# A two-layer graph network on one core: POOL keeps only row transfers in the first part, ScalarE copies the weights, VectorE adds the bias of q, and node pieces come at a ratio of 1.4

## The chip, the core and the metric

One core of a Trainium2 chip runs the whole program. TensorE is called PE, VectorE DVE, ScalarE ACT, GpSimd POOL and SyncE SP. Each engine works through its own instruction list strictly in order and waits for the others by semaphores. The metric is the device time of one execution in microseconds (us).

## The reference, cut to what matters

There are 6250 nodes with 256 features each, and 100000 edges sorted by their destination. Layer 0 is a typed attention: every node has one of three types, every edge one of six relations.

```python
h = relu(layernorm(x))
k, q, v = typed_linear(h, Wk, bk), typed_linear(h, Wq, bq), typed_linear(h, Wv, bv)   # weights of the node's type
k_rel = einsum('nhd,rhde->rnhe', k, rel_att)      # 6 relations, 4 heads
v_rel = einsum('nhd,rhde->rnhe', v, rel_msg)
att = (q[dst] * k_rel[edge_type, src]).sum(-1) * rel_pri[edge_type] / sqrt(64)
# softmax over the edges of one (destination, relation), weighted sum of v_rel, mean over relations
# then: typed linear, skip, layernorm, residual; layer 1 is a GAT on the same edges, batchnorm, elu, residual
```

The change is in the part that makes q, k_rel and v_rel for all nodes while the edges are sorted.

## The kernel before, in words

The first part does two things side by side. `sort_edges` (line 619) sorts the edges by destination and relation, almost wholly on DVE: exchanges of minimum and maximum (lines 686 and 687) in rows of an array, and, from step k = 8 on, in its columns as well. Between the two layouts the array is turned by seven PE transposes (`turn`, line 710, transposes at line 713). The sort is a Python generator: it yields a cost after each group of steps, and right after issuing a `turn`.

`node_stage` (line 588) handles the nodes in blocks of 128 rows that are sorted by node type, 51 blocks (SB). It is a generator too. One turn of its loop has five pieces, each ending in a `yield` with its cost. I call them A to E:

- A: gather the rows of a block eleven ahead (`take_rows`, POOL, line 482), copy a block's k and v weights to a fixed place (`take_weights`, POOL, line 490), the row statistics on DVE (`row_scales`, `row_stats`), and `relate(s, 0)`.
- B: `relate(s, 1)`. C: `keys_values(s + 1)`, 16 matmuls (line 543) and four ACT evictions (line 549). D: `relate(s, 2)`.
- E: `relate(s, 3)`, ending in the scatter of the block's k_rel and v_rel rows to memory (POOL, line 447); the normalized rows of block s + 3 (ACT, line 522); the transpose of block s + 2 (line 530); and `queries(s + 1)`: two PE products (line 557) into a PSUM bank, the copy of the bank by ACT (line 562), the addition of the bias by POOL (line 563), and the scatter of the q rows (line 447).

Each `relate` is eight matmul records on PE (line 577, for two parts together) and one ACT copy of 128x768 from PSUM (line 578). `bank()` gives PSUM banks from a pool of two: keys_values, the transpose and the queries use them in turn.

The order of the work is the order in which this Python code issues it (`tc.manual_schedule()`): nothing is reordered in the first part. The two generators are woven by this loop at line 893, in which RATE sets how many node pieces follow each group of sort steps:

```python
        RATE = 1.13
        due = done = 0.0
        for cost in sort_edges():
            due += cost * RATE
            while done < due:
                part = next(nodes, None)
                ...
                done += part
        ...
        for _ in nodes:          # what is left of the nodes
            pass
```

So in every engine's list the order around one turn is: the transposes of the turn, then the node pieces that are due, then the sort steps that work on what was turned. I call that a segment. There are 24 turns. The message stage after it (`chain`, `bulk`, lines 1034 and 1216) loads the q rows back into `QA` (`load_queries`, line 942), whose memory is also the staging room of k_rel and v_rel, and gathers from `kv_d`: it needs all nodes and the whole sort.

Of the kernel before, what the change touches and what calls it, by code (L numbers as in the profile page):

```python
# [8 lines left out]
F32 = mybir.dt.float32  # L9
# [3 lines left out]
OP = mybir.AluOpType  # L13
# [4 lines left out]
P = 128  # L18
# [6 lines left out]
def kernel(  # L25
# [29 lines left out]
    nc = tc.nc  # L55
    N, D = x.shape
# [4 lines left out]
    FC = D // P  # L61
# [159 lines left out]
    with ExitStack() as st:  # L221
# [4 lines left out]
        nwork = st.enter_context(tc.tile_pool(name="nwork", bufs=2))  # L226
# [5 lines left out]
        def bank():  # L232
            return ps_n.tile([P, 512], F32, name="nps")
# [50 lines left out]
        w_s = nconst.tile([P, FC, T, 3, D], F32, name="w_s")  # L284
# [5 lines left out]
        bq_s = nconst.tile([P, T, D], F32, name="bq_s")  # L290
# [88 lines left out]
        for t in range(2, T):  # L379
# [20 lines left out]
            op=OP.is_equal,  # L400
# [7 lines left out]
        for j in range(0, NX, 7):  # L408
# [5 lines left out]
                op=OP.is_equal,  # L414
# [30 lines left out]
        def scatter(table, to, index, key):  # L445

            i = nc.gpsimd.indirect_dma_start(  # L447
                out=table,
                out_offset=bass.IndirectOffsetOnAxis(ap=index, axis=0),
                in_=to,  # L450
                in_offset=None,
                bounds_check=table.shape[0] - 1,
                oob_is_err=False,
            )
            tc.declare_no_dep(i.ins, group=key, reason="each row is written once")
            tc.add_to_no_dep_group(key, i.ins)


        GN = 4
        xbs, mvs, rss, hqs, hTs, ws, kvs, kinds = {}, {}, {}, {}, {}, {}, {}, {}  # L460
        PE, POOL = mybir.EngineType.PE, mybir.EngineType.Pool

        def kind_of(b, engine):
            if (engine, b) not in kinds:
                n = min(8, SB - b)
                _, ks = nc.values_load_multi_w_load_instructions(
                    kind_i[0:1, b : b + n],
                    engines=[engine],
                    min_val=0,
                    max_val=T - 1,  # L470
                    skip_runtime_bounds_check_because="a block is of one of T types",
                )
                kinds.update({(engine, b + i): k for i, k in enumerate(ks)})
            return bass.ds(kinds[engine, b], 1)

        def there(b):
            return 0 <= b < SB

        def take_rows(b):
            if there(b):  # L480
                xbs[b] = nwork.tile([P, D], F32, name="xb", bufs=10)
                nc.gpsimd.indirect_dma_start(
                    out=xbs[b], out_offset=None, in_=x[:, :],
                    in_offset=bass.IndirectOffsetOnAxis(ap=from_row[:, b : b + 1], axis=0),
                )

        def take_weights(b):
            if there(b):
                ws[b] = nwork.tile([P, FC, 2, D], F32, name="w_now")
                nc.gpsimd.tensor_copy(  # L490
                    ws[b].rearrange("p c i d -> p c (i d)"),
                    w_s[:, :, kind_of(b, POOL), 1:, :].rearrange("p c a i d -> p c (a i d)"),
                )

        def row_stats(b):
            if not there(b):
                return
            g, i = b // GN, b % GN
            if i == 0:
                mvs[g] = nwork.tile([P, GN, 2], F32, name="mv_n", bufs=3)  # L500
                rss[g] = nwork.tile([P, 2, GN], F32, name="rs_n", bufs=3)
            st = nwork.tile([P, nc.vector.BN_STATS_DIM], F32, name="st_n")
            nc.vector.bn_stats(out=st, in_=xbs[b])
            nc.vector.bn_aggr(out=mvs[g][:, i, :], in_=st)
            if i == GN - 1 or b == SB - 1:
                nc.scalar.activation(rss[g][:, 0, : i + 1], mvs[g][:, : i + 1, 1], AF.Sqrt, bias=eps_t)

        def row_scales(b):
            if there(b) and b % GN == 0:
                n = min(GN, SB - b)  # L510
                rs, mv = rss[b // GN], mvs[b // GN]
                nc.vector.reciprocal(rs[:, 0, :n], rs[:, 0, :n])
                nc.vector.scalar_tensor_tensor(
                    rs[:, 1, :n], mv[:, :n, 0], -1.0, rs[:, 0, :n], op0=OP.mult, op1=OP.mult
                )
# [18 lines left out]
        def keys_values(b):  # L534

            if not there(b):
                return
            kv = bank().rearrange("p (i n) -> p i n", n=P)
            w = ws.pop(b)
            for i in range(2):  # L540
                for c in range(FC):
                    for ci in range(FC):
                        nc.tensor.matmul(
                            kv[:, i * FC + c, :], w[:, ci, i, c * P : (c + 1) * P], hTs[b][:, ci, :],
                            start=(ci == 0), stop=(ci == FC - 1),
                        )
            kvs[b] = nwork.tile([P, 2 * FC, P], F32, name="kvT")
            for i in range(2 * FC):
                nc.scalar.activation(kvs[b][:, i, :], kv[:, i, :], AF.Identity, bias=bias_c[:, i, b : b + 1])

        def queries(b):
            if not there(b):
                return
            q = bank()[:, :D]
            hT = hTs.pop(b)
            for c in range(FC):
                nc.tensor.matmul(
                    q, hT[:, c, :], w_s[:, c, kind_of(b, PE), 0, :].rearrange("p a d -> p (a d)"),
                    start=(c == 0), stop=(c == FC - 1),
                )  # L560
            hq = hqs.pop(b)
            nc.scalar.copy(hq[:, 1, :], q)
            nc.gpsimd.tensor_tensor(
                hq[:, 1, :], hq[:, 1, :], bq_s[:, kind_of(b, POOL), :].rearrange("p a d -> p (a d)"), op=OP.add
            )
            scatter(hq_d[:, :], hq.rearrange("p i d -> p (i d)"), to_row[:, b : b + 1], "hq")

        def relate(b, part):

            if not there(b):  # L570
                return
            i, c = part // FC, part % FC
            rel = room[:, b % 4 * RB : (b % 4 + 1) * RB].rearrange("p (r i h e) -> p r i h e", r=R, i=2, h=H)
            ps = ps_r.tile([P, 2, 512], F32, name="rps")[:, :, : R * DK].rearrange("p a (r e) -> p a r e", r=R)
            for a in range(2):
                rows = slice(a * DK, (a + 1) * DK)
                nc.tensor.matmul(ps[:, a], kvs[b][rows, i * FC + c, :], (ra_s, rm_s)[i][rows, c], start=True, stop=True)  # L577
            nc.scalar.copy(rel[:, :, i, 2 * c : 2 * c + 2, :].rearrange("p r h e -> p h r e"), ps)  # L578
            if part == 3:
                del kvs[b]  # L580
                scatter(
                    kv_d.rearrange("(n r) d -> n (r d)", r=R),
                    room[:, b % 4 * RB : (b % 4 + 1) * RB],
                    to_row[:, b : b + 1],
                    "kv",
                )

        def node_stage():

            for s in range(-11, SB):  # L590
                take_rows(s + 11)
                take_weights(s + 2)
                row_scales(s + 3)
                row_stats(s + 9)
                relate(s, 0)
                yield 0.9 * there(s)
                relate(s, 1)
                yield 0.9 * there(s)
                keys_values(s + 1)
                yield 2.1 * there(s + 1)  # L600
                relate(s, 2)
                yield 0.9 * there(s)
                relate(s, 3)
                norm_rows(s + 3)
                turn_rows(s + 2)
                queries(s + 1)
                yield 0.9 * there(s) + 0.45 * there(s + 2) + 1.1 * there(s + 1)

        nodes = node_stage()

        for n in (3, 3, 0, 0, 0, 0, 1, 1, 4, 4, 4):
# [278 lines left out]
            )  # L890
            nc.vector.tensor_tensor(dl0, keyc, dlf[:, :NT], op=OP.mult)

        RATE = 1.13
        due = done = 0.0
        for cost in sort_edges():
            due += cost * RATE
            while done < due:
# [81 lines left out]
    with ExitStack() as st:  # L979
# [4 lines left out]
        op = st.enter_context(tc.tile_pool(name="a0o", bufs=2))  # L984
# [469 lines left out]
    with ExitStack() as st:  # L1454
# [5 lines left out]
        op = st.enter_context(tc.tile_pool(name="b1o", bufs=2))  # L1460
# [270 lines left out]
        with tc.manual_schedule():  # L1731
# [19 lines left out]
            for c in range(DENSE):  # L1751
                ahead = chain(c + 1) if c + 1 < DENSE else iter(())
                soon = destination_scores(c + 2) if c + 2 < DENSE else iter(())
                for j in range(C):
                    t = c * C + j
                    i = t // GT
# [40 lines left out]
    with ExitStack() as st:  # L1797
# [71 lines left out]
        for k in range(PC):  # L1869
            for c in range(FC):  # L1870
                d = hT[:, c, k * PW : (k + 1) * PW]
                nc.vector.tensor_scalar(d, d, mu[:, c : c + 1], None, op0=OP.subtract)
        for k in range(PC):
            for c in range(FC):
                d = hT[:, c, k * PW : (k + 1) * PW]
# [87 lines left out]
```

## Time and profile before

| | us |
|---|---|
| median of 3 runs | 3434.46 (3433.5 to 3435.92) |
| the profiled execution, its own time | 3434.26 |
| its span | 3432.4 |
| first turn of the sort begins | 139.8 |
| last sort instruction on DVE ends (L891) | 430.8 |
| last scatter of k_rel and v_rel leaves POOL (L447) | 496.1 |
| first product of the message stage on PE (L1074) | 545.9 |

The profile's times count from the start of its span. A row of the waits names the engine and line that waited, what released it, the total, the number of waits and the longest. A row of the timeline has start, duration, engine, line, operation and, in brackets, the idle time before it. The granted clock of PE (PEclk) is a share of full speed.

### The profile page before, as it was taken

Reading aid. Unit: us, or ns where it says so; the run is one execution under the profiler, and the core shown is the slowest. Engines: PE = TensorE matmul, PEld = TensorE weight load, DVE = VectorE, ACT = ScalarE, POOL = GpSimd, SP = SyncE. Lnnn points to the kernel's source line nnn. Section 1 sums busy time; section 2 is a strip of 40 time slices with the busy share of each in tenths; the row PEclk is TensorE's granted clock in tenths of the full one; section 3 lists DMA queues with packets and bytes.
Section 4 is the critical chain, followed back from the end, with each engine's and each line's share of the span. In section 5 each row is a group of like instructions: output and inputs, shape, how many; then the busy total and the mean of one; then the engine's idle time right before and its main releaser. Section 6 shows DMA issues by size and latency. Waiting matters only on the chain. (4 is left out here: it accounts for less than half of the span.)

```text
span 3432.4 us, 45921 instructions
## 1 busy us (share of the span) xinstructions
PE 2286.5 (67%) x9977; PEld 1621.8 (47%) x9977; DVE 2431.4 (71%) x5405; ACT 1924.1 (56%) x7430; POOL 2138.1 (62%) x2156
## 2 busy tenths in 40 slices
PE   3888874787777777777776775265555555655554
PEld 2555543555555555555544664144333334434343
DVE  8999714898888989889876886255555555555576
ACT  5656560776767778677784442244444444444446
POOL 4656545677666666667623443777777777777730
PEclk9899886998989999999998997577787777787786
DMA  3555688777667766667725663444444444444434
GB/s 105 224 203 225 208 269 222 210 213 210 183 188 209 214 207 194 185 210 212 209 88 144 180 182 114 133 130 122 127 128 121 124 126 126 125 126 125 112 89 137
DMA packets 262728, 571.40 MB, mean 166 GB/s; under 512 B 65779, under 2 KB 161193, under 8 KB 256194
## 3 DMA queue, kind: packets, MB, share of 16 engines
q0 software_dynamic: 124368, 444.93, 42.4%
q1 hardware_dynamic: 130454, 116.55, 12.4%
q10 hardware_dynamic: 7622, 6.83, 0.8%
q8 instruction: 94, 1.54, 0.2%
q14 instruction: 190, 1.56, 0.2%
HBM read 458.03 MB, written 114.06 MB: 167 GB/s over the span
## 5 line engine op out<-in xcount | busy, mean ns | idle before, releaser
L971 POOL DMA_INDIRECT ring<-kv_d,idx x832 | 819.3, 985 | 442.3 <-ACT wrows L1230 187.4
L971 POOL DMA_INDIRECT rows<-xw_d,idx x832 | 873.9, 1050 | 260.8 <-issue 201.4
L1230 ACT ACTIVATE wrows<-ring,wt 128x64 f32<-128x64 f32 x3328 | 834.1, 335 | 0.1
L1713 PE MATMUL aps<-wrows,ebn 128*128 128x264 f32 x1664 | 590.3, 495 | 318.4 <-DVE ebn L1689 164.5
L1074 PE MATMUL qe<-QA,nbe 128*128 x1664 | 475.2, 420 | 172.2 <-DVE nbe L1059 99.9
L1295 PE MATMUL aps<-wrows,ebn 128*128 128x258 f32 x1664 | 517.9, 420 | 39.6 <-ACT wrows L1230 32.2
L1713 PEld LDWEIGHTS aps<-wrows,ebn 128*128 128x128 f32 x1664 | 343.5, 233 | 398.8 <-ACT wrows L1675 348.3
L1074 PEld LDWEIGHTS qe<-QA,nbe 128*128 128x128 f32 x1664 | 334.4, 209 | 269.1 <-issue 166.3
L1675 ACT ACTIVATE wrows<-rows,ex 128x64 f32<-128x64 f32 x1664 | 434.2, 336 | 0.0
L1295 PEld LDWEIGHTS aps<-wrows,ebn 128*128 128x128 f32 x1664 | 317.0, 205 | 132.4 <-ACT wrows L1230 80.2
L1086 DVE TENSOR_TENSOR pr<-ring,qe 128x512 f32<-128x512 f32 x416 | 277.7, 679 | 136.3 <-PE qe L1074 72.3
L1532 ACT COPY asr<-rows 128x16 f32<-128x16 f32 x208 | 44.7, 216 | 575.0 <-DMA rows<-xw_d,idx 574.9
L1729 DVE TENSOR_TENSOR acc<-acc,aps 128x264 f32 x416 | 177.1, 426 | 181.4 <-PE aps L1713 165.8
L1089 DVE TENSOR_REDUCE att<-pr 128x8 f32<-128x512 f32 x416 | 268.9, 678 | 0.1
L1239 DVE SCALAR_TENSOR_TENSOR QA<-QA,same,aps 128x258 f32 x416 | 194.5, 468 | 42.4 <-PE aps L1295 38.4
L578 ACT COPY QA<-rps 128x768 f32<-128x768 f32 x204 | 164.1, 804 | 87.8 <-PE rps L577 84.9
L1577 DVE TENSOR_TENSOR e<-asr,ad 128x128 f32<-128x128 f32 x26 | 10.1, 389 | 218.1 <-ACT asr L1532 218.1
L1390 PE MATMUL nps<-wa_s,tm 128*128 128x256 f32 x600 | 145.2, 394 | 9.4 <-DMA hbuf<-hq_d 6.4
L447 POOL DMA_INDIRECT kv_d<-QA,to_row x51 | 56.7, 1112 | 143.1 <-ACT QA L578 137.0
L1208 DVE TENSOR_TENSOR ebn<-ifree,dl 128x512 f32<-128x512 f32 x208 | 140.9, 678 | 3.7 <-DMA hq_d<-hq,to_row 1.9
L1689 DVE TENSOR_TENSOR ebn<-ifree,dl 128x512 f32<-128x512 f32 x208 | 142.6, 686 | 0.0
L1682 DVE TENSOR_TENSOR wrows<-rows,ex 128x512 f32<-128x512 f32 x208 | 142.0, 683 | 0.4
(437 smaller groups left out, 3869.3 us busy)
## 6 DMA issues: line engine op xcount, KB each, us to landing
near<-row_d SPq DMA_DIRECT2D x208, 128.0 KB
near<-row_d SPq DMA_DIRECT2D x52, 512.0 KB
ring<-kv_d,idx POOLq DMA_INDIRECT x832
rows<-xw_d,idx POOLq DMA_INDIRECT x832
keeps<-prev_d SPq DMA_DIRECT2D x416, 16.0 KB
r<-r_d SPq DMA_DIRECT2D x12, 512.0 KB
out_dram<-y SPq DMA_DIRECT2D x12, 512.0 KB
xw_d<-xw SPq DMA_DIRECT2D x49, 113.8 KB
```

What stands on the lines that cost most here:

```text
L578: nc.scalar.copy(rel[:, :, i, 2 * c : 2 * c + 2, :].rearrange("p r h e -> p h r e"), ps)
L971: nc.gpsimd.indirect_dma_start(out=to, out_offset=None, in_=table[:, :], in_offset=bass.IndirectOffsetOnAxis(ap=index, axis=0))
L1074: nc.tensor.matmul(qe[:, i, :], oh[j // GT][:, j % GT + i, :], QA[:, 1:, :D][:, bass.ds(bs[j // 2], 1), :].rearrange("p a d -> p (a d)"), ...
L1086: nc.vector.tensor_tensor(pr.rearrange("p t h e -> p t (h e)"), ring[:, lane : lane + 2, slot(t), :], qe, op=OP.mult)
L1089: nc.vector.tensor_reduce(att[:, :, k + j : k + j + 2].rearrange("p h t -> p t h"), pr, AX.X, OP.add)
L1230: nc.scalar.activation(wv[:, j % GT, cols], v[:, cols], AF.Copy, scale=w[:, h, j : j + 1])
L1239: nc.vector.scalar_tensor_tensor(a, a, same[:, t : t + 1], sums.pop(j), op0=OP.mult, op1=OP.add),
L1295: nc.tensor.matmul(sums[j - j % 2], hot[j // GT][:, j % GT, :], wvs[j // GT][:, j % GT, :], start=(j % 2 == 0), stop=(j % 2 == 1),)
L1390: nc.tensor.matmul(tr, m[:, t, c, :], wa_s[:, t, c, :], start=(t == 0 and c == 0), stop=(t == T - 1 and c == FC - 1),)
L1675: nc.scalar.activation(wv[:, part, h, :DK], rows[:, part, h, :DK], AF.Copy, scale=ex[:, 0, h, g * GT + part : g * GT + part + 1],)
L1713: nc.tensor.matmul(sums[t - t % 2], oh[:, t % GT, :], wv[:, t % GT].rearrange("p h e -> p (h e)"), start=(t % 2 == 0), stop=(t % 2 == 1),)
L1729: nc.vector.tensor_tensor(a, a, sums.pop(t).rearrange("p (h e) -> p h e", h=H), op=OP.add)
```

## The change

POOL keeps the row gathers and scatters only. The weights of a block are copied by ACT in two halves of 128x512, one in piece A and one in piece D. The bias of q is added by DVE, straight from the PSUM bank, in a new function `queries_out`, which piece A calls for the block whose products the piece E before it issued; the scatter of the q rows moves along. ACT's copy of the bank goes. RATE is 1.4.

```diff
-        PE, POOL = mybir.EngineType.PE, mybir.EngineType.Pool
+        PE, ACT, DVE = mybir.EngineType.PE, mybir.EngineType.Activation, mybir.EngineType.DVE
...
-        def take_weights(b):
+        def take_weights(b, c):
             if there(b):
-                ws[b] = nwork.tile([P, FC, 2, D], F32, name="w_now")
-                nc.gpsimd.tensor_copy(
-                    ws[b].rearrange("p c i d -> p c (i d)"),
-                    w_s[:, :, kind_of(b, POOL), 1:, :].rearrange("p c a i d -> p c (a i d)"),
+                if c == 0:
+                    ws[b] = nwork.tile([P, FC, 2, D], F32, name="w_now")
+                nc.scalar.copy(
+                    ws[b][:, c].rearrange("p i d -> p (i d)"),
+                    w_s[:, c, kind_of(b, ACT), 1:, :].rearrange("p a i d -> p (a i d)"),
                 )
...
+            qs[b] = q
+
+        def queries_out(b):
+            if not there(b):
+                return
             hq = hqs.pop(b)
-            nc.scalar.copy(hq[:, 1, :], q)
-            nc.gpsimd.tensor_tensor(
-                hq[:, 1, :], hq[:, 1, :], bq_s[:, kind_of(b, POOL), :].rearrange("p a d -> p (a d)"), op=OP.add
+            nc.vector.tensor_tensor(
+                hq[:, 1, :], qs.pop(b), bq_s[:, kind_of(b, DVE), :].rearrange("p a d -> p (a d)"), op=OP.add
             )
             scatter(hq_d[:, :], hq.rearrange("p i d -> p (i d)"), to_row[:, b : b + 1], "hq")
...
             for s in range(-11, SB):
                 take_rows(s + 11)
-                take_weights(s + 2)
                 row_scales(s + 3)
                 row_stats(s + 9)
                 relate(s, 0)
+                queries_out(s)
+                take_weights(s + 2, 0)
                 yield 0.9 * there(s)
                 relate(s, 1)
                 yield 0.9 * there(s)
                 keys_values(s + 1)
                 yield 2.1 * there(s + 1)
                 relate(s, 2)
+                take_weights(s + 2, 1)
                 yield 0.9 * there(s)
                 relate(s, 3)
                 norm_rows(s + 3)
                 turn_rows(s + 2)
                 queries(s + 1)
                 yield 0.9 * there(s) + 0.45 * there(s + 2) + 1.1 * there(s + 1)
...
-        RATE = 1.13
+        RATE = 1.4
```

## The prediction

> **What bounds the kernel now.** The change touches only the first part, so I read the busy slices for where it ends, then a table of two of its stretches, the waits, and the timeline.
>
> ```profile
> span 3432.4 us, 45921 instructions
> ...
> DVE  8999714898888989889876886255555555555576
> ```
>
> A slice is 86 us. DVE is at 7 to 9 tenths in the first five slices and at 1 in the sixth: the sort sets the pace until about 430 us.
>
> ```profile
> core 0: us, PE busy (x) PEld busy (x) DVE busy (x) ACT busy (x) POOL busy (x), PEclk, DMA share, GB/s
> 139.80:430.80 291.00, 246.84 (x1416) 163.81 (x1415) 258.96 (x439) 173.30 (x366) 173.75 (x165) 0.91 0.58 217
> ...
> 434.00:490.00 56.00, 55.96 (x342) 36.75 (x341) 1.39 (x4) 46.30 (x100) 32.91 (x35) 1.00 0.85 296
> ```
>
> From the first turn of the sort to its last instruction DVE works 259 of 291 us. Then it stops, and PE alone is full (55.96 of 56) with the node blocks that were left over: 65 us, to 496.1. The first product of the message stage comes 49.8 us after that, at 545.9, when q has been loaded back.
>
> ```profile
> POOL kv_d L447 <- ACT QA L578: 137.0, 46, 12.5
> ...
> DVE kind_at L931 <- PE nps L926: 44.9, 1, 44.9
> ...
> PE turn L713 <- DVE sort_s L687: 29.4, 11, 5.2
> ...
> DVE sort_s L747 <- PE turn L713: 6.0, 7, 1.3
> ```
>
> The third and fourth rows matter most: PE waits for the sort (29.4), DVE hardly waits for PE. DVE needs nothing of the node pieces, so PE's pieces and DVE's sort steps of a segment run side by side.
>
> **Relief of DVE.**
>
> ```profile
> 87.05 0.62 DVE L687 TENSOR_TENSOR sort_s<-sort_s 128x448 f32<-128x448 f32 x1
> ...
> 88.25 1.94 DVE L687 TENSOR_TENSOR sort_s<-sort_s 128x448 f32<-128x448 f32 x1
> 88.64 1.06 POOL L490 COPY w_now<-w_s 128x1024 f32 x1
> ```
>
> The same exchange takes 0.62 us alone and 1.94 us where POOL's weight copy meets it. I summed what DVE instructions took above the usual time of their form: 37.9 us between 139.8 and 430.8, and 12.9 before, and each of the long ones overlaps L490 or L563, none the row transfers alone. Both POOL instructions go, so I take all of it off. The other bound is 0, if the row transfers, which stay, are what blocks.
>
> The Trainium skill (SBUF — State Buffer, "Who interferes with whom") says that a DVE instruction with two SBUF inputs and a POOL instruction that reads SBUF exclude each other for their whole length. The row fits it.
>
> **Block pace on PE.** The tail shows an undisturbed block.
>
> ```profile
> 453.05 1.56 PE L577 MATMUL rps<-ra_s,kvT 64*128 64x384 f32 x8
> 454.54 2.05 PE L543 MATMUL nps<-hT,w_now 128*128 128x128 f32 x16
> 456.53 1.56 PE L577 MATMUL rps<-rm_s,kvT 64*128 64x384 f32 x8
> 458.02 0.44 PE L530 MATMUL nps<-ident,hq 128*128 128x128 f32 x2
> 458.29 1.03 PE L557 MATMUL nps<-w_s,hT 128*128 x4
> ```
>
> The next block starts at 459.25. Start to start: A and B 0.745 each, C 1.99, D 0.745, E 1.975 (0.745 + 0.27 + 0.96); a block is 6.20.
>
> **ACT.** In the tail it idles 0.97 us of each 6.20 waiting for L543, so it works 5.23. It loses the bank copy (0.38, of which 0.27 start to start) and gains two 128x512 copies, a form the trace does not have as a copy. Between 128x256 at 0.41 (L1645) and 128x512 with scale and bias at 0.80 (L1904) I take 0.55, by the slope of the copies L532 and L578 (0.36 for 256, 0.80 for 768). Block: 5.23 - 0.27 + 1.10 = 6.06, still under PE. With 0.80 each it is 6.56 and ACT sets the pace.
>
> **The added wait on DVE.** The addition reads PE's product. Its place decides. In the built program DVE's list has, in one segment, statistics and additions first and then the sort steps; PE's has the turn, then all node pieces. So whenever a segment holds a piece E followed by its A, DVE stands at the addition until PE has run the pieces up to that E, and the sort steps queue behind it. PE cannot do those pieces earlier: they lie behind the turn, which needs the sort steps before. Side by side becomes one after the other.
>
> I replayed the loop on RATE by its costs and added the PE time from the turn to the last E whose A is in the same segment. For example, the segment D E A B C D E A gives 0.745 + 1.975 + 4.225 + 1.975 = 8.9. The 24 segments at 1.4, in order: 0, 8.9, 0, 6.2, 2.0, 8.2, 2.7, 8.2, 2.7, 6.2, 8.2, 8.9, 11.7, 5.5, 6.2, 6.2, 14.4, 5.5, 12.4, 8.9, 10.9, 6.2, 8.2, 4.7. Sum 162.8. At 1.13 it would be 99.9.
>
> Each of the 22 waits ends in one addition on the path. Nearest rows: 0.47 (L1239, 128x258, address from a register) and 0.43 (L1729, from PSUM). With the semaphore I take 0.5: 11. The other additions run while DVE waits anyway.
>
> **Cold turns.** While DVE sorts after its wait, PE has only the rest of the pieces and then idles, 4 us and more in 15 of the segments.
>
> ```profile
> 237.54 1.76 PE L713 MATMUL turn<-ident,sort_s 128*128 128x128 f32 x7 [3.87 <-DVE sort_s L687]
> ...
> 249.70 0.93 PE L713 MATMUL turn<-ident,sort_s 128*128 128x128 f32 x7
> ```
>
> After 3.87 us of idling the seven transposes take 1.76 instead of 0.93, and the next matmuls are slow too (four of L577 1.65 for 0.92, sixteen of L543 2.85 for 2.05). That is 0.83 + 0.73 + 0.80, some 2.3 per cold turn: 15 x 2.3 = 35. A second row in the trace turned cold after 2.96, one after 3.08 did not, so the count may be 8 to 22: 18 to 51 us.
>
> The Trainium skill (TensorE: Matmul & The Clock Gate, "Why this matters for your kernels") warns of idle gaps over about 3 us between bursts, and this change makes such gaps the rule. By its half clock for a window of 3.4 us a gap would cost 1.7, so 26 for the 15, as an estimate.
>
> **The sum.** Sort, from the first turn: DVE's 258.9 less 21.6 of node statistics, which now fall into the waits, less 37.9 = 199.4; 24 turns at 1.0 = 24; waits 162.8; additions 11; cold 35; one segment where PE's pieces outlast the sort steps, 1. Total 433, where 291 stood. Ahead of the first turn there are no transposes to tie the engines; 12.9 goes off DVE, some 10 additions (5) and a few waits come, so I leave 139.8. The sort ends at 573.
>
> In that time all 51 blocks are issued, so the tail is gone. The last pieces after the last addition take PE 6.2, then the ACT copy 1.6 and POOL's scatter 1.1: the last scatter leaves about 4 us after the sort, at 577. Before, 496.1: 81 later. Behind it I keep the 49.8 us. POOL's and SP's small loads of types and norms, which were done at 445, now follow the last scatter, but the built list of SP puts the first q load right after them and ahead of the loads of `keeps`; plus or minus 5. POOL loses 1.05 + 0.8 per block, which costs and gains nothing by itself: it waited 137 us for ACT.
>
> 3434.3 (profiled execution, 0.2 under the median) + 81 = 3515.
>
> **Rivals.**
>
> Rival 1, faster: PE keeps ahead and DVE finds q done. Then the relief counts. DVE would need 199.4 + 24 + 41 blocks x 1.17 (statistics 0.67, addition 0.5) = 271; PE 41 x 6.2 + 24 x 0.95 + half the cold = 254 + 23 + 17 = 294, and bounds. Last scatter at 139.8 + 294 + 3 = 437, 59 earlier: 3375. For it: POOL and DVE are clearly relieved and the 65 us tail is real. Against it: the order in the lists. It decides where waits, additions and cold turns, 209 in all, shrink below 128 (209 - 81).
>
> Rival 2: the waits come, but the blocking of DVE stays, because the row transfers hold DVE as well: 38 more, 3553. Against it: no long exchange meets a row transfer alone.
>
> Rival 3: the waits come and ACT sets the pace at 6.56: 162.8 is 26.3 blocks, x 0.36 = 9 more, 3524; it moves the number, not the sign.
>
> **How the numbers follow.** Forecast 0.76, rival 2 0.06, rival 3 0.06, rival 1 0.09, something near no change 0.03. A measurement of this kernel can tell about 0.2% from no change, 7 us. Low end: cold 18 instead of 35, additions and the stretch ahead of the first turn 10 less, the end 5 less, and 10 for waits that come out shorter than my piece times: 3473. High end: cold 51, ACT 9, half of rival 2 19, the end 5: 3564. Rival 1 is left out. Faster 0.09, same 0.03, slower 0.88.
>
> **What would show it.** Right: DVE waits for L557's products of 150 to 200 us in total, while L686 and L687 fall from 0.71 to 0.83 us to about 0.62; a granted clock under 0.86 in the sort; no stretch with PE alone; the last scatter of k_rel and v_rel at 555 to 600. Wrong: DVE's waits for PE under 100 us, or that scatter before 496.

## The result and the profile after: 4.0% slower

The changed kernel takes 3572.5 us (median of 4, 3562.7 to 3575.28) where the kernel before takes 3435.19 on the same chip: a ratio of 1.0399, 95% interval 1.0376 to 1.0423. The forecast was 3515 with a range to 3564: right in sign, 57.5 us short, and 8.5 above the upper end. The profiled execution took 3562.7, 128.4 more than that of before; its span is 3560.9. It is the fastest of the four, so the table accounts for 128.4 of the 137.3 us between the medians.

| stage, us | before | after | difference | forecast |
|---|---|---|---|---|
| up to the last scatter of k_rel and v_rel (its start) | 495.1 | 578.0 | +82.9 | +81 |
| from there to the first product of the message stage | 50.7 | 59.4 | +8.7 | 0 (±5) |
| message stage, first to last product | 1269.2 | 1316.2 | +47.0 | 0 (not named) |
| rest of the span | 1617.4 | 1607.3 | -10.1 | 0 (not named) |

So the part that was reasoned through came out within 2 us (in part by luck, see below). The time that was missed lies in stages in which the change edits nothing.

The slices of the page, a slice now being 89 us:

```profile
span 3560.9 us, 45949 instructions
...
PE   3876773588777777777777677345665555656554
...
DVE  7764552698889898878876788445555555555576
```

DVE, at 7 to 9 in the first five slices before, is down to 4 to 6 in the third to sixth, and PE never has a slice to itself. The table of stretches (first turn to the end of the first part; the message stage):

```profile
core 0: us, PE busy (x) PEld busy (x) DVE busy (x) ACT busy (x) POOL busy (x), PEclk, DMA share, GB/s
...
140.30:579.20 438.90, 314.41 (x1717) 206.36 (x1715) 233.14 (x480) 237.18 (x491) 116.27 (x114) 0.85 0.49 175
...
637.40:1953.60 1316.20, 1008.27 (x3738) 706.22 (x3738) 1103.50 (x2429) 895.91 (x3945) 807.53 (x820) 0.90 0.63 187
```

In the sort no engine is full: PE works 314 of 439 us, DVE 233, ACT 237. PE's and DVE's times add up to only 1.25 times the stretch (1.74 before, where 246.84 and 258.96 stood in 291.00): the two mostly take turns. The waits of that stretch say at what (waiting line, releaser, total, number, longest):

```profile
POOL kv_d L447 <- ACT QA L584: 290.5, 41, 18.3
DVE hq L569 <- PE nps L559: 188.4, 34, 8.9
...
PE turn L721 <- DVE sort_s L695: 84.6, 14, 11.5
...
PE turn L721 <- DVE cols L695: 25.5, 4, 12.3
```

The second row did not exist before; the third stood at 29.4. POOL's 290 us cost nothing by themselves: it waits for rows that PE and ACT make late. One segment shows both halves. First DVE in the timeline:

```profile
249.95 0.18 DVE L506 BATCH_NORM_AGGREGATE mv_n<-st_n 128x2 f32<-128x6 f32 x1
254.80 0.42 DVE L569 TENSOR_TENSOR hq<-nps,bq_s 128x256 f32<-128x256 f32 x1 [4.67 <-PE nps L559]
255.14 0.62 DVE L690 TENSOR_SCALAR sign_c<-gray_t 128x896 int32<-128x896 int32 x1
255.79 1.09 DVE L746 TENSOR_TENSOR sort_s<-turn,sign_c 128x896 int32<-128x896 int32 x1
```

The turn had been done since 251.1, and DVE could have begun to sort; the addition stands ahead of it in its list and waits 4.67 us for the products of L559. Then PE, two segments on:

```profile
275.13 0.92 PE L583 MATMUL rps<-rm_s,kvT 64*128 64x384 f32 x4
281.14 1.75 PE L721 MATMUL turn<-ident,sort_s 128*128 128x128 f32 x7 [5.09 <-DVE sort_s L695]
282.82 1.65 PE L583 MATMUL rps<-rm_s,kvT 64*128 64x384 f32 x4
284.41 0.69 PE L532 MATMUL nps<-ident,hq 128*128 128x128 f32 x2
284.89 1.91 PE L559 MATMUL nps<-w_s,hT 128*128 x4
```

PE idles 5.09 us until DVE has sorted, then the turn takes 1.75 (0.93 elsewhere) and the four products of L559 take 1.91 (1.03 in the undisturbed block shown ahead of the prediction).

The gains that the change was made of came too. The groups of DVE in the sort (busy time, mean ns of one):

```profile
L694 DVE TENSOR_TENSOR sort_s<-sort_s 128x448 f32<-128x448 f32 x60 | 37.6, 626 | 2.0
L695 DVE TENSOR_TENSOR sort_s<-sort_s 128x448 f32<-128x448 f32 x60 | 37.1, 618 | 0.0
```

Before, the same two groups had means of 725 and 843 ns:

```profile
L687 DVE TENSOR_TENSOR sort_s<-sort_s 128x448 f32<-128x448 f32 x60 | 50.6, 843 | 0.0
L686 DVE TENSOR_TENSOR sort_s<-sort_s 128x448 f32<-128x448 f32 x60 | 43.5, 725 | 2.1
```

Last the message stage. Its row in the table of stretches before, to set beside the last row above:

```profile
545.80:1815.00 1269.20, 978.39 (x3738) 694.70 (x3738) 1096.21 (x2429) 898.04 (x3945) 807.84 (x820) 0.92 0.65 194
```

Its waits before:

```profile
POOL ring L971 <- ACT wrows L1230: 187.4, 175, 7.2
...
ACT wrows L1225 <- PE aps L1295: 104.3, 55, 12.4
PE qe L1074 <- DVE nbe L1059: 99.9, 51, 5.9
```

and after:

```profile
POOL ring L979 <- ACT wrows L1238: 220.6, 157, 16.5
...
ACT wrows L1233 <- PE aps L1303: 168.8, 56, 16.5
PE qe L1082 <- DVE nbe L1067: 135.0, 64, 7.6
```

The instructions and their counts are the same (3738 on PE, 2429 on DVE, 3945 on ACT, 820 on POOL in both), DVE's and ACT's busy times agree within 8 us, but the engines wait longer for one another. Only the first part is issued in the written order; behind it the lists are ordered when the program is built. Set side by side row by row, the two built programs differ there: PE's, DVE's and ACT's lists in more than a hundred places each, SP's in some ten, POOL's in none. The order in which the two profiles show the instructions differs in the same way. The places that the build gives the tiles in memory are the same in both. The change moved the order of work that it does not touch. Whether that is the cause had to be tested.

### The profile page after: what moved, and what is told of

It reads as the page before. It is cut to its first block, busy times and chain, and to the rows that moved or that the text cites. A ratio compares the mean times of both kernels' runs of the same rounds, so it can differ in the third digit from the quotient of the medians.

```text
span 3560.9 us, 45949 instructions
## 1 busy us (share of the span) xinstructions
PE 2342.4 (66%) x9977; PEld 1645.6 (46%) x9977; DVE 2404.0 (68%) x5456; ACT 1950.6 (55%) x7481; POOL 2030.6 (57%) x2054
## 3 DMA queue, kind: packets, MB, share of 16 engines
q8 instruction: 94, 1.54, 0.2%
## 5 line engine op out<-in xcount | busy, mean ns | idle before, releaser
L979 POOL DMA_INDIRECT ring<-kv_d,idx x832 | 819.0, 984 | 498.9 <-ACT wrows L1238 220.6
L1721 PE MATMUL aps<-wrows,ebn 128*128 128x264 f32 x1664 | 604.1, 503 | 297.9 <-ACT wrows L1683 159.9
L1303 PE MATMUL aps<-wrows,ebn 128*128 128x258 f32 x1664 | 532.3, 434 | 44.5 <-ACT wrows L1238 32.0
L1721 PEld LDWEIGHTS aps<-wrows,ebn 128*128 128x128 f32 x1664 | 346.4, 236 | 381.5 <-ACT wrows L1683 332.0
L1303 PEld LDWEIGHTS aps<-wrows,ebn 128*128 128x128 f32 x1664 | 321.6, 211 | 155.6 <-ACT wrows L1238 98.9
L569 DVE TENSOR_TENSOR hq<-nps,bq_s 128x256 f32<-128x256 f32 x51 | 21.7, 425 | 206.7 <-PE nps L559 192.0
L1585 DVE TENSOR_TENSOR e<-asr,ad 128x128 f32<-128x128 f32 x26 | 10.1, 389 | 210.5 <-ACT asr L1540 210.5
L1561 PEld LDWEIGHTS <-near 128*128 128x128 bf16 x832 | 97.1, 118 | 101.7 <-issue 42.7
L1697 DVE TENSOR_TENSOR ebn<-ifree,dl 128x512 f32<-128x512 f32 x208 | 143.2, 689 | 0.0
```

What stands on the lines that cost most here:

```text
L979: nc.gpsimd.indirect_dma_start(out=to, out_offset=None, in_=table[:, :], in_offset=bass.IndirectOffsetOnAxis(ap=index, axis=0))
L1303: nc.tensor.matmul(sums[j - j % 2], hot[j // GT][:, j % GT, :], wvs[j // GT][:, j % GT, :], start=(j % 2 == 0), stop=(j % 2 == 1),)
L1697: nc.vector.tensor_tensor(oh, ifree[:, None, :].to_broadcast([P, GT, P]), dl[:, i * GT : (i + 1) * GT, None].to_broadcast([P, GT, P]), op= ...
L1721: nc.tensor.matmul(sums[t - t % 2], oh[:, t % GT, :], wv[:, t % GT].rearrange("p h e -> p (h e)"), start=(t % 2 == 0), stop=(t % 2 == 1),)
```

## The experiments

Theory A: the message stage is as long as its lists make it, and the first part follows the order of waits that the prediction described. Theory B: the later first part (another clock, later transfers, other memory traffic) lengthens the message stage. The kernels ran on four chips, and the message stage differs between chips far more than the change moves it (the kernel before: 3435.19, 3985.89, 3951.84 and 3431.55 us), so stages are compared within a chip, except those of the first part, which agree from chip to chip (the kernel before reaches its last scatter at 495.1 and 497.7). Times of the sort's end and of the last scatter are from here on the starts of these instructions.

**1 and 2. The same lists on both sides.** A fence ahead of the load of q is a mark in the program across which the build moves no instruction. With it both kernels have the same lists behind the mark (DVE's differ in the place of one memset):

```diff
         nc.vector.memset(QA[:, :, D:], 0.0)
+        tc.no_sync_barrier()
```

For the kernel before:

> The kernel before, with a fence for the scheduler alone behind the first part, so that the built lists of the message stage are the same in all kernels that carry it. Both theories: the first part as before, last scatter of k_rel and v_rel at 494 to 498 us. The message stage may be a few per cent longer or shorter than the 1269 us of before, since its lists change. This is the base for the fenced kernels.

For the changed kernel:

> The changed kernel with the same fence. Theory A (the first part loses by DVE's waits, and the other 47 us come from the scheduler, which wrote other lists for the message stage): last scatter at 575 to 583, message stage within 6 us of the fenced kernel before, total 80 to 98 us above it. Theory B (the same message stage runs slower because of how the changed first part leaves DMA queues, clock or memory): the message stage is 35 to 55 us longer although its lists are the same, total 125 to 145 above.

Measured, on one chip: 4044.64 for the kernel before with the fence (ratio to the kernel before without it 1.0123, interval 1.0074 to 1.0171) and 4130.2 for the changed kernel with it (1.0356, 1.0324 to 1.0388), 85.6 more. The message stages, in this order:

```profile
542.40:2246.20 1703.80, 1127.05 (x3738) 761.88 (x3738) 1110.97 (x2429) 907.13 (x3945) 801.99 (x820) 0.80 0.49 145
```

```profile
636.10:2335.80 1699.70, 1107.16 (x3737) 747.05 (x3738) 1111.61 (x2429) 905.42 (x3945) 803.00 (x820) 0.81 0.49 145
```

With the same lists the changed kernel's message stage is no longer than the other's (-4.1), though its first part still ends 84.2 us later (582.1 against 497.9). And the fence alone costs the kernel before 58.7 us, while its first part is unchanged: 497.9 against 497.7 without it on another chip. The rest of the span, whose lists are the same too, is 17.7 us shorter in the second profile, so a difference of a few us between two profiles says nothing; theory B asked for 35 to 55, and falls.

**3. The addition out of the way.** The changed kernel with ACT copying the bank again, and DVE adding the bias in place only at the head of the next segment, seven buffers of `hq` instead of five, fenced:

```diff
-            qs[b] = q
+            nc.scalar.copy(hqs[b][:, 1, :], q)
+            pend.append(b)
...
-                queries_out(s)
...
         for cost in sort_edges():
             due += cost * RATE
+            queries_out()
```

> The changed kernel with the fence and the same number of additions on DVE, but each addition is issued behind the sort steps of its segment: ACT copies the bank out, DVE adds in place at the head of the next segment. Theory A (the place of the addition costs, not the addition): DVE's waits for PE fall from 192 us to under 30, the last scatter leaves at 435 to 465, total 30 to 60 us under the fenced kernel before. Rival (DVE's added work, or ACT's weight copies, are what costs): last scatter stays over 540, total 40 us or more above it.

Measured: 4006.96 (ratio 1.0053, 1.0029 to 1.0076), 37.7 under run 1. The sort ends at 446.9 instead of 580.7, the last scatter leaves at 454.4 instead of 582.1; the message stage takes 1688.1, 12 to 16 less than in runs 1 and 2. DVE's wait ahead of the additions in the sort:

```profile
DVE hq L574 <- ACT hq L563: 33.6, 9, 6.5
```

Of 199.8 us of waiting for PE in run 2, 33.6 (for ACT) are left. RATE, the weights on ACT and the addition on DVE are as in the changed kernel; what differs is that the bank is copied by ACT and DVE adds a segment later, and 128 us go with it. L694 and L695 have the same mean here as in the changed kernel (626 and 618 ns).

**4. The weights on ACT, the rest as before, RATE 1.4**, fenced:

```diff
-                take_weights(s + 2)
...
                 relate(s, 0)
+                take_weights(s + 2, 0)
...
                 relate(s, 2)
+                take_weights(s + 2, 1)
...
-        RATE = 1.13
+        RATE = 1.4
```

> The kernel before with the fence, the weight copies on ACT and RATE 1.4, while the copy of the bank stays on ACT and the bias on POOL: nothing of the nodes' products is on DVE. Theory A: no new wait on DVE, two thirds of the blocking (L490's part, some 35 of 51 us) gone, last scatter at 440 to 465, total 30 to 55 us under the fenced kernel before. Rival (ACT cannot carry the weight copies): last scatter at 480 or later.

Measured: 4037.3 (ratio 1.0111, 1.0076 to 1.0146). Last scatter at 462.4, 35.5 ahead of run 1, with the same lists behind it; message stage 1703.9. ACT's copies take 655 ns each (51.8 us for 79). The total, expected 30 to 55 us under run 1, is only 7.3 under it (medians of four executions each, which spread over 17 and 33 us). In the two profiles 7.0 of the 35.5 go again between the last scatter and the first product (51.4, where run 1 has 44.5), and 11.6 behind the message stage, for which no run shows a cause.

**5 to 8. The unfenced pair again, and another kind of fence** (a barrier that all engines wait at), on one chip:

> The kernel before, unchanged, for its profile on the chip of this call. First part as on record: last scatter at 493 to 499 us. Theory A (lists): its message stage is shorter than that of the changed kernel on this chip by 30 to 70 us, and differs from that of the kernels with a barrier as well.

> The changed kernel, unchanged, timed on the chip of this call. Last scatter at 575 to 585 us on any chip, since the first part waits on engines and not on memory. Theory A: its message stage is 30 to 70 us longer than that of the kernel before, with other lists. If the stage were longer only because of what the first part leaves behind (theory B), the two kernels with a barrier would show the same difference.

> The kernel before with a barrier of all engines behind the first part: a third set of lists for the message stage, the same in both kernels with the barrier. Last scatter at 493 to 499. Both theories: message stage of some length M.

> The changed kernel with the same barrier, and so the same lists in the message stage. Last scatter at 575 to 585. Theory A: message stage within 8 us of that of the other kernel with the barrier. Theory B: 30 to 70 us longer.

Unfenced, the changed kernel is slower again: 4073.62, ratio 1.0291 (1.024 to 1.0343). The kernel before reaches its last scatter at 497.7 and has a message stage of 1620.2; the changed one 579.7 and 1659.7: +82.0 and +39.5. With the barrier in both (one execution each, 4016.28 and 4115.22; the last scatter of the kernel before at 500.4, just outside the expected 493 to 499), 1680.8 and 1670.4: the changed kernel's is 10.4 shorter, a little more than the expected bound from one profile each, and on the other side. So two kinds of fence agree: with the same lists the message stage of the changed kernel is not longer.

**9. The one edit that pays: weights on ACT at RATE 1.13, unfenced.** The diff of run 4 without its RATE and its fence. Its lists behind the first part are those of the kernel before, row for row.

> The kernel before with one edit: ACT copies the weights in two halves, as in the changed kernel; the bank copy (ACT), the bias addition (POOL) and RATE 1.13 stay. Its lists behind the first part are those of the kernel before, row for row. Theory A (DVE waits only where it reads PE's products; the later stages follow their lists): DVE's waits for PE in the sort stay under 20 us; of the 37.9 us by which POOL's instructions held DVE some 15 to 25 go; the last scatter of k_rel and v_rel leaves at 470 to 485 (497.9 before); the message stage is as long as before's on this chip; ratio 0.990 to 0.995. Theory B (the first part's longer load on ACT or PE's clock decides the message stage too): last scatter about 500, ratio 1.000 to 1.010.

Measured: 3399.7 (3386.07 to 3403.59) against 3431.55, ratio 0.9914 (0.9893 to 0.9934): faster than both kernels. Last scatter at 459.7, 35.4 earlier than in the profile of before and 10 below the expected range: the first turn comes 10 us earlier (129.7), and from there the sort takes 264.2 us where it took 291.0.

```profile
507.20:1768.90 1261.70, 975.75 (x3737) 694.89 (x3738) 1095.44 (x2429) 897.89 (x3945) 807.45 (x820) 0.92 0.65 195
```

With before's lists the message stage keeps before's length (1269.2 in the first profile, taken where the kernel before has a median of 3435.19 instead of 3431.55). The profiled execution is the fastest of the six, 13.6 under the median.

**10. The arithmetic of the wait at another RATE.** The changed kernel with RATE 1.13, fenced:

> The changed kernel with the fence ahead of the load of q, and RATE put back to 1.13. Theory A (a wait lasts as long as the PE pieces that lie between the turn and the product read): by the replay of the loop the waits are 99.9 us at 1.13 where they are 162.8 at 1.4; what was measured at 1.4 stands 11% above that replay, so DVE waits 105 to 125 us for L557's products, the sort ends at 505 to 530, and since some ten blocks are left over behind it, the last scatter leaves at 560 to 595, as late as at 1.4. Theory B (the waits come from PE's pace per block): waits go by blocks issued in the sort, 41 of 51, 150 to 160 us, sort end 540 to 555, last scatter about 610.

```profile
DVE hq L569 <- PE nps L559: 135.4, 24, 8.5
```

That is the wait from the first turn to the end of the sort (130.8 to 505.5), in one execution of 3591.85 us. It is outside the expected 105 to 125, and 36% above the replayed 99.9 (188.4 is 16% above 162.8, not 11% as the expectation has it). The bare replay leaves out the cold products and the additions. With them it holds at both rates: 15 turns of this run took 1.64 us or more, so 99.9 + 15 x 1.53 + some 21 additions of 0.5 make 133, and from the end of each turn to the first sort step behind it the 24 segments take 138.1 us. Theory A scaled the cold turns down with the waits, but there are as many of them here. The wait does fall with the rate, the sort ends at 504.4, and the left-over blocks follow, so the last scatter leaves at 570.8, hardly earlier: with the addition where it is, a faster sort leaves a tail, and the sum hardly changes.

**11 and 12. RATE alone.** The kernel before with RATE 1.4 as its only edit, with the fence and without:

> The kernel before with the fence ahead of the load of q, and RATE 1.4 alone: POOL still copies the weights and adds the bias, ACT copies the bank. Theory A (the order only costs where DVE reads PE's product): DVE's waits for PE stay under 20 us, the 65 us of left-over blocks are gone, the sort ends at 455 to 475 because all 51 blocks' statistics and POOL copies meet it, and the last scatter leaves within 10 us of it, at 462 to 485. Theory B (all node pieces ahead of the sort steps hold DVE by themselves): sort end 540 to 580.

> The kernel before with RATE 1.4 as its only edit, no fence: the lists of all engines but POOL behind the first part come out otherwise than at 1.13, though nothing there is edited. Theory A (the message stage follows its lists): the first part is that of the fenced run with RATE 1.4 within 8 us, and the message stage differs from that of the run with the weights on ACT, which has before's lists, by more than 15 us, in either direction. Theory B (the message stage does not care for the order): it differs by less than 10 us.

Fenced (one execution, 3528.29), the sort ends at 485.5 and the last scatter leaves at 493.1, each some 10 us later than expected. What I had not foreseen is a wait of DVE for the gathered rows:

```profile
L503 DVE BATCH_NORM_STATS2 st_n<-xb 128x6 f32<-128x256 f32 x34 | 14.2, 418 | 43.0 <-DMA xb<-in_x_dram,from_row 43.0
```

6.3 us before. Run 4 has 45.8 of it without POOL's weight copy, so it comes with the rate. Unfenced (one execution, 3463.21), the last scatter leaves at 487.5 (5.6 from the fenced run), and the message stage, on one chip with run 9, is

```profile
541.40:1842.20 1300.80, 991.72 (x3737) 698.37 (x3738) 1100.34 (x2429) 897.69 (x3945) 811.13 (x820) 0.91 0.64 189
```

1300.8: 39 longer than run 9's 1261.7, with 8 us gained ahead of it. The fenced runs 10 and 11 of that chip have 1362.4 and 1369.0. So one chip shows three sets of lists and three lengths, 1262, 1301 and 1362 to 1369, and the two kernels that share a set agree within 7 us. That a changed RATE gives other lists for all engines but POOL is seen in the built programs: run 9 and the kernel before share theirs at 1.13, and the kernel with RATE 1.4 has neither theirs nor those of the changed kernel.

## Why the prediction was right and wrong

**The added wait (162.8) and the cold turns (35).** Right in mechanism and in size. A cold turn was counted as 0.83 in the transposes and 1.53 in the products behind them, and these lie inside the wait. From the end of each turn to the first sort step behind it the 24 segments take 199.1 us in the profile; for that stretch the sum has 162.8 + 11 + 15 x 1.53 + 1 = 197.8. (The 188.4 of the waits is DVE's idling alone, without the statistics that run in these stretches.) It holds segment by segment: the two replayed at 0 took 0.3 and 0.0, the longest, replayed at 14.4, took 17.6; only the last, 4.7, took 0.8. 13 of 24 turns took 1.75 or 1.76 and two 1.54 and 1.24. The granted clock in the sort fell to 0.85, as foretold. Run 3 shows that the place of the addition makes the wait; run 10 that the replay holds at another rate once its cold turns are counted.

**Relief of DVE (37.9).** Right. The six largest groups of exchanges sum to 178.2 us before and 143.2 after, L682 (now L690) 9.9 and 6.5: 38.4. The sort's own DVE time was put at 199.4; it is 194.0 (233.1 less 21.7 of statistics and 17.4 of additions). With the row transfers still on POOL the exchanges are at 0.62, so rival 2 falls. That the weight copy is a large part of it: at RATE 1.4 DVE is busy 267.8 us in the sort with POOL's copy (run 11) and 231.8 with ACT's (run 4).

**The rule of the Trainium skill (SBUF — State Buffer, "Who interferes with whom")**, that a two-input DVE instruction and a POOL instruction that reads SBUF shut each other out, fits the exchanges. L682, which also came down (992 to 647 ns), has one SBUF input only, so this sentence of the page does not cover it. The rule told which instructions to take off POOL, and not what their new place would make DVE wait for.

**ACT (0.55 a copy).** Mis-sized, without effect. The copies take 0.65 on average, so a block is 5.23 - 0.27 + 1.30 = 6.26 and no longer under PE's 6.20. But in the sort ACT waits 148.2 us for the products of `relate`, so rival 3 is not what happened.

**The sort (433).** It ends at 578.3 (573 forecast). The last scatter starts at 578.0 and ends at 579.2 (577 forecast), so the sort came 5 us late and the scatter followed it about 3 us sooner than the 4 that were allowed: that the two nearly cancel is luck. Rival 1, in which DVE finds q done, is not this kernel, but run 3 is a kernel of that kind: last scatter at 454.4, where the rival put 437.

**"Behind it I keep the 49.8 us."** The first of the two steps that failed, by 8.7. The reason given, that SP's list has the load of q ahead of the loads of `keeps`, does not hold in the profile (SP's built list has the profile's order, so it was misread):

```profile
589.04 7.67 SPq L1047 DMA_DIRECT2D keeps<-prev_d  x8
596.82 0.28 SPq L914 DMA_DIRECT2D ntr_i<-in_node_type_dram  x1
...
599.22 1.29 SPq L1063 DMA_DIRECT2D near<-row_d  x2
602.37 0.34 SPq L954 DMA_DIRECT2D QA<-hq_d  x1
```

Before, where the types and norms had been loaded by 445:

```profile
498.90 0.79 SPq L1039 DMA_DIRECT2D keeps<-prev_d  x2
...
509.01 0.43 SPq L946 DMA_DIRECT2D QA<-hq_d  x1
```

SP waits 21.1 us for the last q rows to land, until 589.0, 11 us after the last scatter of k_rel and v_rel begins (498.9, 3.8 after it, before); then come eight loads of `keeps` and seven of types and norms. The first load of q goes out 24.3 after that scatter's start, where it was 13.9. Of these 10.4 us, 7.2 are the later landing; why the rows land later is open.

But the place of `keeps` is not what costs. In the fenced kernels the first load of q does stand ahead of them, as the prediction had it, and the distance from the last scatter to the first product grows all the same: 44.5 in run 1 and 54.0 in run 2. It goes with RATE. At 1.4 the fenced kernels have 51.4 to 54.0 (runs 2, 3, 4 and 11, whichever engine adds), at 1.13 44.5 and 45.2 (runs 1 and 10). At 1.13 the loads of types and norms go out while the left-over blocks run. At 1.4 there is no such tail: they go out behind the last scatter and ahead of q, whose first load follows that scatter after 12.4 us in run 2, 2.2 in runs 1 and 10. In run 2:

```profile
583.38 0.30 SPq L914 DMA_DIRECT2D ntr_i<-in_node_type_dram  x1
...
594.52 0.33 SPq L955 DMA_DIRECT2D QA<-hq_d  x1
```

The prediction saw that these loads now follow the last scatter and gave them no time of their own beyond the plus or minus 5.

**What stood behind it, at no change.** The second step that failed, and the one that broke the range. The prediction begins "The change touches only the first part"; its sum ends at the first product and adds the rest of the 3434.3 unread, with neither a term nor an end of the range for it. +47.0 in the message stage came from lists that were reordered when the program was built (runs 1, 2, 7 to 9 and 12). The built lists, of which the prediction reads nothing behind SP's load of q, have the differing rows, but nothing here turns such rows into a time: one reordering cost 39 us (run 12), the fence 59 in the whole span (run 1). Which of the differing rows costs the time, and why the rest of the span came out 10.1 shorter (4.4 shorter on the next chip, 19.3 longer with the barrier in both), stays open.

## What to carry to other kernels

An operation that reads another engine's product is priced by what is queued behind it: here additions of 0.42 us each held the sort for 188 us in all, because they stood ahead of work that was ready; the same additions a segment later, from a copy that ACT had made, cost a sixth of that. And where a build orders part of a program by itself, an edit elsewhere can reorder it: compare the built lists of the whole program, and where they differ, put the length of that stage into the range. To judge an edit by itself, fence the stage or find a form that leaves its lists alone: the weights on ACT gave 35 us of first part at RATE 1.13 (495.1 to 459.7) and 31 at 1.4 (493.1 to 462.4), and run 9, whose lists are those of before, brought its gain to the end of the span (31.9 of it). And work that runs in the shadow of a tail, such as the small loads here, is to be priced when the tail goes.

## What the runs showed of the hardware that was not expected

The four chips run the same program at 3432 to 3986 us. The difference sits in the stages that gather: the first part reaches the last scatter at 495.1 and 497.7, while the message stage takes 1269.2 on one and 1620.2 on another, with DVE busy 1096 and 1104 us in it and the DMA engines 0.65 and 0.51. Nothing here tells why.

Idle PE did not turn cold by one length. In the profile after, all gaps of 5.09 us and more were followed by a turn of 1.75 or 1.76, gaps of 2.97 to 3.21 by turns of 0.98 to 1.24, and one of 1.95 by 1.54. Before, a gap of 2.96 was followed by 1.69, three of 3.07 to 3.23 by 0.98.
